# Gathering the slots' rows of h by indirect DMA instead of by a product with a selection matrix, in a four-layer graph kernel

## The chip, the cores and the metric

The kernel runs on one core of a Trainium2 chip. The metric is the device time of one execution in microseconds (us). Runs of one kernel agree within about 0.3%.

## What is computed

The inputs are node features `x` (8 batches, 2048 nodes, 64 features), a sparse row-normalised 2048 x 2048 matrix `adj`, a hypergraph membership matrix `H` (2048 nodes, 64 edges) and weights. Four layers follow each other, each as x = layernorm(x + layer(x)). The change lies in layer 1, cut here to what matters:

```python
h = x @ W
agg = einsum('ben,bnf->bef', alpha, h)              # one row per edge
beta = sigmoid((h @ a_gn)[:, None, :] + (agg @ a_ge)[:, :, None])
all_he = elu(beta * h + (1 - beta) * agg)           # node x edge pairs, where H > 0
industry = einsum('nm,bmf->bnf', adj / deg, x @ W_ind)
g = einsum('bne,benf->bnf', coefs1, all_he)         # sum over the edges of a node
out = softmax-weighted sum of industry and g        # then residual and layernorm
```

Layer 0 is a polynomial in `adj` with weights of its own per node, layers 2 and 3 are products with `adj` and small matrices.

## The kernel before

**Tiles.** The 2048 nodes are 16 tiles of 128. A row of a node holds all 8 batches x 64 features, 512 numbers, so a tile of features is 128 x 512. `j` is the tile. Matrices with `adj` are done as a 0/1 mask times a high and a low part of the features (fp32r), 32 matmuls of 128x512 a tile.

**Stages.** First product (0 to about 140 us of the span), layer 0 (to about 650), the head of layer 1 (650 to 663), its 16 tiles interleaved with each other and with layer 2's projections (663 to about 930), layer 2, layer 3.

**Units of a node.** Most nodes belong to one to three edges. A tile therefore handles four units of 128 rows each: the first, second and third edge of every node, and a fourth unit of up to 128 *slots* in which further edges of any node of the tile are listed. `S[:, j, :]` is the 0/1 matrix from nodes to slots of tile `j`; `oh` holds the 0/1 matrices from edges to the rows of each unit. Both are built in the first product by `memberships` (steps interleaved between matmuls, with one PSUM bank `li`), kept in device memory, and loaded again in layer 1.

**Steps of layer 1.** For tile `j`, `units` gives: `sx` (TensorE: gate sums and the transpose of S), `ST`, `gates`, `tau` (sigmoids `sig` and `rest`), `ch0`/`ch1` (GpSimd: sig x h, for units 0 and 1, and for unit 2), `gp0`/`gp1` (TensorE: agg of each unit, two units each), `m0`/`m1` (VectorE: times `rest`), `z0`/`z1` (VectorE: sum), `exp0`/`exp1` (ScalarE), `e0`/`e1` (VectorE: elu), `w0`/`w1` (GpSimd: times coefficient), `a0`, `ga` (GpSimd) and `red` (TensorE: slots back to nodes), `g` (VectorE). For the fourth unit the kernel before does it otherwise than for the others: `dp` (TensorE) forms h of the slot's node minus agg of its edge by two products, with S in full fp32 and with `nagg` = -agg; `t3` (ScalarE, eight pieces) multiplies this by `sig`; `m1` leaves the fourth unit out; `z1` adds agg. `mixer` holds what follows `g` (`tr`, `sT`, `fc`, `th`, `sub`, `df`, `rw`, `rt`, `mult`, `r`, `s`, `centre`, `sq`, `var`, `rstd`, `x2`), `layer2` the projections (`f`, `xT`, `mm`, `hi`, `add`, `lo`), and `industry` the mask loads (`mask`), eight portions `i` of four matmuls for each tile, and `ind`.

**Order.** Inside `program_order` every compute engine runs its instructions in the order in which they are written. For layer 1 that order is a list of some 1000 tokens (`3.gp0` is step `gp0` of tile 3) which `perform` walks through; a shorter list, `head`, orders the part on edges before it. TensorE's portions `i` are spread between the steps. SP's queue carries nearly all DMAs, in its own order, and its instructions wait in line. PSUM: `g` and `fc` have one buffer of two banks each, `m` two buffers, `sm` one.

**Lines.** L954, L955 `dp`; L960 `t3`; L944 `m`; L947 `z`; L966 `e`; L971 `w`; L925 `ch`; L936 `gp`; L985 `red`; L807 the products with `pT` in the head (`dnp`, `dnp2`); L1937 the industry products; L709, L710 the loads of `pT` and S; L1599 ScalarE's copy of `h`; L538 a write of 2048 numbers to device memory by GpSimd's queue (`s_row`).

Of the kernel before, what the change touches and what calls it, by code (L numbers as in the profile page):

```python
# [13 lines left out]
ALU = mybir.AluOpType  # L14
# [49 lines left out]
def kernel(  # L64
# [242 lines left out]
    s_row = scr.tile([1, N], F32, tag="s_row", name="s_row")  # L307
    lists = {
# [8 lines left out]
    def memberships(pre, ps, pm, fcw_sb, fcb_sb, fcg_sb):  # L317
# [23 lines left out]
        nc.gpsimd.tensor_scalar(iota[:, 1, :], iota[:, 0, :], 4.0, None, op0=ALU.add)  # L341
        cnt3, base3, end3 = (
# [34 lines left out]
        for q in range(NQ):  # L377
# [19 lines left out]
            S = pre.tile([P, 4, P], F32, tag="S", name=f"S_{q}")  # L397
            yield
            for t in range(4):
# [16 lines left out]
                for h in range(2):  # L416
                    nc.vector.scalar_tensor_tensor(
                        r_(rk[:, h, :]), sm[:, 0:E], base3[:, j:j + 1], pm[:, j, :],
                        op0=ALU.add, op1=ALU.mult,
                    )  # L420
# [8 lines left out]
                )  # L429
            store(q, oh23, 2)  # L430
            nc.sync.dma_start(lists["S"][q], S)
# [178 lines left out]
    def layer1(  # L610
# [13 lines left out]
        agg1, nagg = (  # L624
            l1.tile([P, BC], F32, tag=f"agg{i}", name=f"agg_{i}") for i in range(2)
        )
# [17 lines left out]
        def industry(j):  # L644
# [25 lines left out]
            return dict(mask=mask, i=products, ind=scaled)  # L670

        g_of, ind_of, mask_of, acc_of, done_of = {}, {}, {}, {}, {}
# [24 lines left out]
        def column_view(src):  # L697
# [3 lines left out]
            "1.mask 2.mask 3.mask 4.mask 0.i c.hexp c.he 0.ind c.w1 c.trhe c.agg1 c.heT "  # L701
            "c.w2 c.fche c.sums c.the c.nagg 1.i c.sep 1.i c.serow c.sert 1.i c.ese c.eexp c.ese2 "
            "c.dnp c.ext 1.i c.rec c.hgr c.dnp2 1.i c.late "
        )
        with tc.tile_pool(name="fa", bufs=2) as fa:
# [18 lines left out]
            with program_order():  # L724
# [46 lines left out]
                def negated():  # L771
                    full = fa.tile([P, BC], F32, tag="full", name="full", bufs=1)
                    nc.vector.tensor_scalar(full, c["agg"], -1.0, None, op0=ALU.mult)
                    parts(nagg, full)

# [54 lines left out]
                def other_weights():  # L830
# [7 lines left out]
                    agg1=lambda: parts(agg1, c["agg"]), sums=sum_edges, nagg=negated, ese=capped,  # L838
# [22 lines left out]
        def units(j, dst):  # L861
# [79 lines left out]
            def lessen(i):  # L941
                n = 2 - i
                v = by_b(gps[i][:, 0:n])
                nc.vector.tensor_tensor(v, v, per_b(t["rest"], 2 * i, n), ALU.mult)  # L944
# [7 lines left out]
            def dp():  # L952
                t["dp"] = ps_m.tile([P, BC], F32, tag="m", name=f"dp_{j}")
                nc.tensor.matmul(t["dp"], S[:, j, :], h_sb[:, j, :], start=True, stop=False)  # L954
                nc.tensor.matmul(t["dp"], r_(t["oh"][:, 3, :]), r_(nagg), start=False, stop=True)  # L955

            def t3():
                for b in range(B):
                    bc = slice(b * C, (b + 1) * C)
                    nc.scalar.activation(  # L960
                        ds[1][:, 1, bc], t["dp"][:, bc], AF.Copy, scale=t["sig"][:, 3, b:b + 1]
                    )
# [24 lines left out]
            def g():  # L987
# [4 lines left out]
                sx=sx, ST=copy_ST, gates=gates, tau=tau, dp=dp, t3=t3, a0=add0, ga=add1, red=red, g=g  # L992
# [187 lines left out]
        with program_order():  # L1180
            perform(
                (
                    "0.xr 1.xr c.rests 0.sx 0.gp0 0.ST 0.gates 0.gp1 0.tau 1.sx 0.ch0 0.m0 1.i 1.ST "
                    "0.dp 1.gates 0.ch1 0.m1 1.tau 1.i 0.z0 1.ch0 0.t3 1.dp 1.i 0.exp0 0.z1 2.sx "
                    "1.ind 0.e0 0.exp1 2.i 2.gates 1.ch1 2.ST 1.gp0 0.e1 2.tau 2.i 0.w0 1.t3 1.m0 "
                    "1.gp1 2.i 1.m1 0.w1 1.z0 2.i 0.a0 2.i 1.exp0 0.red 1.z1 0.ga 3.sx 1.e0 1.exp1 "
                    "2.dp 0.g 3.ST 2.ch0 2.gp0 1.e1 0.tr0 2.i 0.sT0 2.m0 1.w1 0.tr1 0.fc0 3.gates "
                    "0.sT1 2.z0 3.tau 2.i 2.ch1 0.th0 1.red 1.w0 2.exp0 0.fc1 2.t3 0.dlt 2.i 0.xg "
                    "2.xr 4.sx 0.th1 3.dp 1.a0 4.gates 2.ind 4.ST 0.sub 3.i 1.ga 2.e0 3.i 0.df 1.g "
                    "3.ch0 2.gp1 0.rw 1.tr0 2.m1 0.rt 3.i 1.sT0 2.w0 2.z1 4.tau 1.tr1 3.i 2.exp1 "  # L1190
                    "1.dlt 1.fc0 1.sT1 2.a0 2.e1 3.i 1.th0 0.mult 2.w1 3.gp0 0.r 1.fc1 3.m0 3.ch1 3.i "
                    "1.th1 0.s 2.ga 3.z0 3.t3 3.i 1.sub 1.xg 3.xr 3.i 5.mask 3.exp0 2.red 0.centre "
                    "3.ind 3.e0 1.df 0.sq 4.i 1.rw 2.g 4.ch0 0.var 3.gp1 2.tr0 3.m1 4.i 2.sT0 3.w0 "
                    "3.z1 2.fc0 3.exp1 4.i 2.dlt 0.rstd 2.th0 3.e1 1.rt 4.i 1.mult 2.tr1 2.xg 4.xr "
                    "0.x2 4.gp0 1.r 4.i 3.w1 4.m0 5.sx 2.sT1 1.s 4.i 5.ST 4.z0 4.ch1 4.dp 5.gates "
                    "3.a0 4.exp0 4.i 1.centre 4.t3 3.ga 4.e0 2.fc1 4.i 6.mask 4.w0 1.sq 5.tau 1.var "
                    "4.gp1 4.ind 3.red 4.m1 2.th1 5.ch0 4.z1 6.sx 5.dp 6.ST 2.sub 4.exp1 4.a0 5.i 3.g "
                    "1.rstd 4.e1 3.tr0 5.i 3.sT0 6.gates 5.gp0 4.w1 1.x2 2.df 5.m0 3.tr1 5.i 5.z0 "
                    "5.ch1 2.rw 3.fc0 3.sT1 6.tau 3.dlt 5.exp0 2.rt 4.ga 4.red 5.t3 5.e0 5.i 3.xg "
                    "5.xr 4.g 5.i 3.th0 6.ch0 2.mult 5.gp1 2.r 4.tr0 5.i 5.m1 4.sT0 5.w0 2.s 4.tr1 "  # L1200
                    "5.z1 5.i 4.xg 6.xr 7.sx 2.centre 5.exp1 5.i 7.mask 7.gates 5.a0 7.ST 2.sq 6.dp "
                    "5.e1 7.tau 5.ind 3.fc1 2.var 5.w1 6.gp0 4.sT1 6.i 3.th1 6.m0 6.ch1 5.red 3.sub "
                    "5.ga 6.t3 6.i 6.z0 2.rstd 4.fc0 5.g 6.exp0 6.i 4.dlt 5.dlt 2.x2 5.tr0 6.i 6.e0 "
                    "3.df 7.ch0 5.sT0 6.gp1 3.rw 6.i 4.th0 6.m1 6.z1 3.rt 6.w0 6.i 3.mult 4.fc1 "
                    "6.exp1 3.r 5.xg 7.xr 8.sx 4.th1 6.e1 6.i 6.a0 8.ST 4.sub 7.gp0 6.i 8.mask 6.w1 "
                    "7.m0 5.fc0 6.ind 8.gates 7.ch1 7.i 7.z0 8.tau 4.df 6.ga 3.s 7.exp0 7.i 3.centre "
                    "4.rw 7.dp 7.e0 5.th0 4.rt 7.t3 7.i 7.w0 4.mult 7.gp1 4.r 7.i 3.sq 7.m1 8.ch0 4.s "
                    "5.tr1 7.z1 7.i 5.sT1 5.fc1 7.a0 4.centre 7.exp1 3.var 7.i 5.th1 7.e1 3.rstd "
                    "6.red 4.sq 5.sub 8.gp0 7.w1 7.i 3.x2 8.m0 5.df 6.g 7.i 9.mask 8.ch1 5.rw 8.z0 "
                    "6.tr0 7.ind 7.ga 5.rt 8.dp 4.var 6.sT0 8.exp0 5.mult 6.xg 8.xr 6.fc0 5.r 8.t3 "  # L1210
                    "8.e0 8.i 4.rstd 9.sx 6.th0 5.s 6.dlt 8.gp1 9.ST 8.i 8.w0 5.centre 4.x2 9.gates "
                    "6.tr1 8.i 8.m1 6.sT1 8.a0 8.z1 7.red 9.tau 5.sq 8.i 9.ch0 7.g 8.exp1 5.var 7.tr0 "
                    "8.i 8.e1 7.sT0 7.xg 9.xr 10.sx 9.gp0 8.w1 10.gates 10.ST 9.dp 9.m0 10.tau 6.fc1 "
                    "9.ch1 9.z0 8.red 6.th1 8.ga 8.i 9.exp0 6.sub 5.rstd 11.sx 9.t3 9.e0 8.i 8.g "
                    "7.fc0 10.ch0 11.ST 5.x2 11.gates 9.gp1 8.i 10.mask 9.m1 9.w0 9.z1 11.tau 6.df "
                    "8.ind 7.tr1 8.tr0 6.rw 7.dlt 9.exp1 9.i 9.a0 6.rt 8.sT0 9.e1 9.i 7.sT1 8.xg "
                    "10.xr 7.th0 8.tr1 6.mult 10.gp0 9.w1 6.r 9.i 10.m0 7.fc1 6.s 10.ch1 9.i 8.sT1 "
                    "10.z0 7.th1 9.ga 9.red 6.centre 10.exp0 9.i 7.sub 6.sq 12.sx 10.e0 9.i 12.ST 9.g "
                    "11.ch0 10.gp1 12.gates 9.i 10.m1 9.tr0 6.var 10.w0 8.fc0 7.df 9.sT0 8.dlt 6.rstd "
                    "9.i 11.mask 7.rw 8.th0 7.rt 10.dp 7.mult 9.ind 10.a0 6.x2 7.r 10.i 7.s 8.fc1 "  # L1220
                    "9.dlt 10.t3 7.centre 9.xg 11.xr 10.i 9.tr1 8.th1 10.i 10.z1 11.dp 9.sT1 8.sub "
                    "10.exp1 10.i 7.sq 10.e1 9.fc0 12.tau 7.var 10.w1 11.gp0 10.i 11.m0 8.df 11.ch1 "
                    "11.z0 10.i 8.rw 9.th0 10.ga 8.rt 10.i 8.mult 11.exp0 7.rstd 9.fc1 8.r 11.t3 "
                    "11.e0 10.i 12.mask 8.s 12.ch0 11.gp1 9.th1 8.centre 10.red 10.ind 11.m1 12.dp "
                    "8.sq 9.sub 11.w0 7.x2 11.i 11.z1 13.sx 11.a0 10.g 11.exp1 11.i 13.gates 10.xg "
                    "12.xr 13.ST 10.tr0 11.e1 13.tau 11.i 10.sT0 8.var 11.w1 12.gp0 11.i 12.m0 10.fc0 "
                    "12.ch1 12.z0 11.i 11.ga 12.t3 10.tr1 11.i 10.dlt 8.rstd 12.exp0 11.red 10.sT1 "
# [47 lines left out]
    def layer0(  # L1275
# [334 lines left out]
        def project(j, n):  # L1610
            projected(j, n)
            for what in ("hi", "h", "sc", "lo"):
                copied(j, n, what)
# [1116 lines left out]
```

## Time and profile before

| | |
|---|---|
| runs | 1195.62, 1195.90, 1199.13 us (median 1195.9) |
| profiled execution | 1195.65 us, span 1193.9 us, granted clock 0.997 |
| TensorE busy | 1176.7 us (99%) |
| VectorE busy | 886.7 us (74%) |
| GpSimd busy | 501.5 us (42%) |
| ScalarE busy | 392.4 us (33%) |
| DMA moved | 157.1 MB, mean 132 GB/s |

Busy time is the sum of the instructions' times; matmuls are pipelined, and their records overlap. A wait that the profile shows is the idle time in front of an instruction and what ended it. Stages differ, so shares are read by window.

### The profile page before, as it was taken

Reading aid. Unit: us, or ns where it says so; the run is one execution under the profiler, and the core shown is the slowest. Engines: PE = TensorE matmul, PEld = TensorE weight load, DVE = VectorE, ACT = ScalarE, POOL = GpSimd, SP = SyncE. Lnnn points to the kernel's source line nnn. Section 1 sums busy time; section 2 is a strip of 40 time slices with the busy share of each in tenths; the row PEclk is TensorE's granted clock in tenths of the full one; section 3 lists DMA queues with packets and bytes.
Section 4 is the critical chain, followed back from the end, with each engine's and each line's share of the span. In section 5 each row is a group of like instructions: output and inputs, shape, how many; then the busy total and the mean of one; then the engine's idle time right before and its main releaser. Section 6 shows DMA issues by size and latency. Waiting matters only on the chain.

```text
span 1193.9 us, 19895 instructions
## 1 busy us (share of the span) xinstructions
PE 1176.7 (99%) x7498; PEld 942.9 (79%) x7498; DVE 886.7 (74%) x1678; ACT 392.4 (33%) x1019; POOL 501.5 (42%) x443
## 2 busy tenths in 40 slices
PE   9999999999999999999999999999999999999996
PEld 7878888888888888888887666666667888888885
DVE  4556578898888888888877788988977666665554
ACT  3100102222222222222223567767767311111111
POOL 2000392555555555555511589988860211100000
PEclk9999999999999999999999999999999999999998
DMA  8887653323333332333294223322220423325551
GB/s 288 237 253 226 171 166 100 108 102 116 109 118 117 99 99 101 111 117 116 89 344 127 70 80 106 115 76 93 97 71 1 177 106 134 113 106 177 179 180 66
DMA packets 101992, 157.10 MB, mean 132 GB/s; under 512 B 13057, under 2 KB 64641, under 8 KB 96257
## 3 DMA queue, kind: packets, MB, share of 16 engines
q1 hardware_dynamic: 97088, 151.51, 38.8%
q10 hardware_dynamic: 4368, 4.20, 1.0%
q8 instruction: 61, 1.00, 0.3%
q14 instruction: 43, 0.34, 0.1%
q0 software_dynamic: 432, 0.05, 0.1%
HBM read 117.97 MB, written 37.76 MB: 130 GB/s over the span
## 4 chain that ended last, share of the span: by engine, by line
PE 94%; DVE 3%; DMA 1%; ACT 1%; issue 1%; POOL 0%; SPq 0%; ACTq 0%; DVEq 0%; POOLq 0%
PE pp L1457 27%; PE a L1937 19%; PE ind L1937 10%; PE y1p L567 9%; PE y2p L1411 9%; PE fc L1035 3%; PE yp L2036 1%; PE try L168 1%; PE gp L936 1%; PE trm L168 1%; PE u L1146 1%; PE red L985 1%; PE hp L1582 1%; PE dp L954 1%; DVE r L1468 1%; PE df L691 1%
## 5 line engine op out<-in xcount | busy, mean ns | idle before, releaser
L1468 DVE SCALAR_TENSOR_TENSOR r<-pp,emb_sb,r 128x256 f32<-128x256 f32 x512 | 247.4, 483 | 76.0 <-PE pp L1457 61.8
L1457 PE MATMUL pp<-w_sb,xT 64*128 64x256 f32 x1024 | 155.6, 380 | 1.9 <-DVE r L1468 1.9
L1457 PE MATMUL pp<-w_sb,y2T 64*128 64x256 f32 x1024 | 153.5, 376 | 0.5 <-DVE y2T L1427 0.5
L1457 PE MATMUL pp<-w_sb,y1T 64*128 64x256 f32 x1024 | 153.4, 376 | 0.0
L1323 POOL TENSOR_TENSOR ms<-msk,srow 128x1024 f32<-128x1024 f32 x30 | 76.6, 2553 | 90.1 <-DVE msk L447 90.1
L1457 PEld LDWEIGHTS pp<-w_sb,y2T 64*128 64x128 f32 x1024 | 99.4, 187 | 11.9 <-DVE y2T L1427 0.9
L1457 PEld LDWEIGHTS pp<-w_sb,y1T 64*128 64x128 f32 x1024 | 99.4, 187 | 11.1
L1457 PEld LDWEIGHTS pp<-w_sb,xT 64*128 64x128 f32 x1024 | 95.1, 187 | 14.6 <-issue 4.4
L567 PE MATMUL y1p<-x_hi,m 128*128 128x512 f32 x256 | 103.3, 404 | 0.3 <-ACT x_hi L469 0.3
L567 PE MATMUL y1p<-x_lo,m 128*128 128x512 f32 x256 | 100.4, 392 | 0.2 <-DVE x_lo L470 0.2
L1937 PE MATMUL a<-y_lo,mj_l 128*128 128x512 f32 x240 | 95.0, 396 | 0.0
L1937 PE MATMUL a<-y_hi,mj_l 128*128 128x512 f32 x240 | 95.0, 396 | 0.0
L1411 PE MATMUL y2p<-y_hi,msk 128*128 128x512 f32 x240 | 94.8, 395 | 0.0
L1937 PE MATMUL a<-v_hi,mj_l 128*128 128x512 f32 x240 | 93.9, 392 | 0.0
L1937 PE MATMUL a<-v_lo,mj_l 128*128 128x512 f32 x240 | 93.7, 391 | 0.0
L1411 PE MATMUL y2p<-y_lo,msk 128*128 128x512 f32 x240 | 93.5, 390 | 0.0
L1937 PE MATMUL ind<-y_hi,mj_l 128*128 128x512 f32 x208 | 90.5, 435 | 0.0
L1937 PE MATMUL ind<-y_lo,mj_l 128*128 128x512 f32 x208 | 81.8, 393 | 0.0
L1363 DVE SCALAR_TENSOR_TENSOR ms<-ms,adj 128x1024 f32<-128x1024 f32 x30 | 67.2, 2240 | 0.0
L971 POOL TENSOR_TENSOR ez<-ez,coef 128x1024 f32<-128x1024 f32 x32 | 61.6, 1927 | 11.0 <-DVE ez L966 10.9
L1118 POOL TENSOR_TENSOR r<-r,bias_sb 128x512 f32<-128x512 f32 x14 | 17.9, 1277 | 105.3 <-DVE r L2057 105.3
L1649 POOL TENSOR_TENSOR hs<-h,es 128x512 f32<-128x512 f32 x15 | 15.6, 1043 | 107.9 <-ACT hgr L1621 107.9
(352 smaller groups left out, 2461.5 us busy)
## 6 DMA issues: line engine op xcount, KB each, us to landing
mj_l<-mask SPq DMA_DIRECT2D x44, 1024.0 KB, 5.0
adj<-in_at SPq DMA_DIRECT2D x64, 256.0 KB, 3.7
mask<-msk SPq DMA_DIRECT2D x32, 512.0 KB, 4.6
raw<-in_at SPq DMA_DIRECT2D x31, 512.0 KB, 5.9
oh<-oh SPq DMA_DIRECT2D x32, 128.0 KB, 4.1
xT<-in_xt SPq DMA_DIRECT2D x16, 256.0 KB, 3.1
xs<-in_xn SPq DMA_DIRECT2D x16, 256.0 KB, 2.7
kept<-x SPq DMA_DIRECT2D x16, 256.0 KB, 3.7
```

What stands on the lines that cost most here:

```text
L168: nc.tensor.matmul(dst, src, ident, start=True, stop=True, is_transpose=True)
L567: nc.tensor.matmul(accs[q][jj], r_(m[:, t, jj * P:(jj + 1) * P]), r_(part[:, mt, :]), start=i + h + t == 0 and part is x_hi, stop=i == 3 a ...
L971: nc.gpsimd.tensor_tensor(by_b(ezs[i]), by_b(ezs[i]), per_b(t["coef"], 2 * i, 2), ALU.mult)
L1035: nc.tensor.matmul(fcs[i][:, h, :], fcw_sb[rs], t["sT", i][rs], start=True, stop=True)
L1118: nc.gpsimd.tensor_tensor(b_view(t), b_view(t), bias2_sb.unsqueeze(1).to_broadcast([P, B, C]), ALU.add)
L1323: nc.gpsimd.tensor_tensor(ms, m, srow[j].unsqueeze(1).to_broadcast([P, 8, P]), ALU.mult)
L1363: nc.vector.scalar_tensor_tensor(ms, ms, 1.0, raws[j][h], op0=ALU.mult, op1=ALU.not_equal, accum_out=bad[:, 2 * j + h:2 * j + h + 1],)
L1411: nc.tensor.matmul(acc, r_(msk[j, mt // 8][:, mt % 8, :]), r_(part[:, mt, :]), start=mt == 0 and part is y_hi, stop=mt == NT - 1 and part ...
L1457: nc.tensor.matmul(pp[:, h, pl, :], terms[j][name][rs, 2 * bq + pl], w_sb[rs, k, dq * 4 * C:(dq + 1) * 4 * C], start=k == 0, stop=k == K - 1,)
L1468: nc.vector.scalar_tensor_tensor(rb, ppv[:, :, dd, :], emb_sb[:, j, d:d + 1], rb, op0=ALU.mult, op1=ALU.add)
L1649: nc.gpsimd.tensor_tensor(b_view(hs), b_view(h_sb[:, j, :]), bcast(es[:, j, :]), ALU.mult)
L1937: nc.tensor.matmul(acc, r_(a[:, mt, :]), r_(part[:, mt, :]), start=mt == 0 and part is hi, stop=mt == NT - 1 and part is lo,)
```

## The change

`h` of every tile is also stored in device memory (`h_rows`, 2048 x 512). In `memberships`, one of the two equal halves of `rk` becomes the node's number, so that the product that gives the edge ranks of the slots also gives, in its first row, the node of each slot; ScalarE writes these as integers, and they are kept in device memory as `slot_row`. Layer 1 loads them as `slot_of`, and a new step `hg` lets GpSimd's queue fetch the 128 rows of a tile's slots by an indirect DMA into one of two buffers. `dp` and `nagg` are gone, `t3` reads the fetched rows, and `m1` multiplies both of its units by `rest`. Both lists of steps are other ones. The core of the diff:

```diff
+    slot_row = scr.tile([1, N], mybir.dt.int32, tag="slot_row", name="slot_row")
+    h_rows = scr.tile([N, BC], F32, tag="h_rows", name="h_rows")
...
+        node = pre.tile([P, 1], F32, tag="node", name="node")
+        nc.gpsimd.iota(
+            node, pattern=[[0, 1]], base=0, channel_multiplier=1,
...
                 rk = pre.tile([P, 2, E], F32, tag="rk", name=f"rk_{j}")
-                for h in range(2):
-                    nc.vector.scalar_tensor_tensor(
-                        r_(rk[:, h, :]), sm[:, 0:E], base3[:, j:j + 1], pm[:, j, :],
-                        op0=ALU.add, op1=ALU.mult,
-                    )
+                nc.vector.tensor_copy(r_(rk[:, 0, :]), node.to_broadcast([P, E]))
+                nc.vector.scalar_tensor_tensor(
+                    r_(rk[:, 1, :]), sm[:, 0:E], base3[:, j:j + 1], pm[:, j, :],
+                    op0=ALU.add, op1=ALU.mult,
+                )
...
+                nc.scalar.activation(
+                    slots[0:1, t * P:(t + 1) * P], sm[0:1, P:2 * P], AF.Copy, bias=float(j * P)
+                )
             store(q, oh23, 2)
+            nc.sync.dma_start(slot_row[:, q * QW:(q + 1) * QW], slots)
...
-        agg1, nagg = (
-            l1.tile([P, BC], F32, tag=f"agg{i}", name=f"agg_{i}") for i in range(2)
-        )
+        agg1 = l1.tile([P, BC], F32, tag="agg", name="agg_1")
+        slot_of = l1.tile([P, NT], mybir.dt.int32, tag="slot", name="slot_of")
+        nc.sync.dma_start(slot_of, slot_row.rearrange("o (t p) -> p (o t)", p=P))
...
+            def slot_rows():
+                rows_of[j] = l1.tile([P, BC], F32, tag="hg", name=f"hg_{j}", bufs=2)
+                nc.gpsimd.indirect_dma_start(
+                    rows_of[j], None, h_rows,
+                    bass.IndirectOffsetOnAxis(slot_of[:, j:j + 1].bitcast(mybir.dt.uint32), 0),
+                )
...
-            "1.mask 2.mask 3.mask 4.mask 0.i c.hexp c.he 0.ind c.w1 c.trhe c.agg1 c.heT "
-            "c.w2 c.fche c.sums c.the c.nagg 1.i c.sep 1.i c.serow c.sert 1.i c.ese c.eexp c.ese2 "
-            "c.dnp c.ext 1.i c.rec c.hgr c.dnp2 1.i c.late "
+            "1.mask 2.mask 3.mask 4.mask 0.hg 0.i c.hexp 1.hg c.he 0.ind c.w1 c.trhe c.agg1 "
+            "c.heT c.w2 c.fche c.sums c.the 1.i c.sep 1.i c.serow c.sert 1.i c.ese c.eexp c.ese2 "
+            "c.dnp c.ext c.dnp2 c.rec c.hgr 1.i c.late "
...
-                n = 2 - i
-                v = by_b(gps[i][:, 0:n])
-                nc.vector.tensor_tensor(v, v, per_b(t["rest"], 2 * i, n), ALU.mult)
+                v = by_b(gps[i])
+                nc.vector.tensor_tensor(v, v, per_b(t["rest"], 2 * i, 2), ALU.mult)
...
-            def dp():
-                t["dp"] = ps_m.tile([P, BC], F32, tag="m", name=f"dp_{j}")
-                nc.tensor.matmul(t["dp"], S[:, j, :], h_sb[:, j, :], start=True, stop=False)
-                nc.tensor.matmul(t["dp"], r_(t["oh"][:, 3, :]), r_(nagg), start=False, stop=True)
...
-                        ds[1][:, 1, bc], t["dp"][:, bc], AF.Copy, scale=t["sig"][:, 3, b:b + 1]
+                        ds[1][:, 1, bc], rows_of[j][:, bc], AF.Copy, scale=t["sig"][:, 3, b:b + 1]
...
+        def kept_rows(j):
+            nc.sync.dma_start(h_rows[j * P:(j + 1) * P, :], h_sb[:, j, :])
```

The list of steps, a piece of it from the middle of tile 4, before and after (all of it is replaced):

```diff
-                    "0.x2 4.gp0 1.r 4.i 3.w1 4.m0 5.sx 2.sT1 1.s 4.i 5.ST 4.z0 4.ch1 4.dp 5.gates "
-                    "3.a0 4.exp0 4.i 1.centre 4.t3 3.ga 4.e0 2.fc1 4.i 6.mask 4.w0 1.sq 5.tau 1.var "
+                    "2.dlt 3.w1 0.var 4.gp0 2.th0 4.i 4.m0 1.rt 4.i 6.mask 4.ch1 4.z0 3.red 0.rstd "
+                    "4.ind 1.mult 4.exp0 5.i 1.r 4.t3 6.sx 4.e0 3.ga 5.i 6.gates 5.ch0 6.ST 4.gp1 "
```

In the new list a gather `j.hg` stands one to two tiles ahead of `j.t3`; `kept_rows(j)` follows the second half of `project(j)` in layer 0, on SP's queue; the load of `slot_of` stands in front of the loads of `pT` and S.

## Prediction before the run

> **What bounds the kernel now.** I read the page's first two parts first: who is busy overall, and whether that changes along the span.
>
> ```profile
> PE 1176.7 (99%) x7498; PEld 942.9 (79%) x7498; DVE 886.7 (74%) x1678; ACT 392.4 (33%) x1019; POOL 501.5 (42%) x443
> ...
> POOL 2000392555555555555511589988860211100000
> ```
>
> TensorE is busy in 99% of the span, so over the whole run work taken off it is time. But the average hides one stage: GpSimd, 42% over the run, stands at 8 to 9 tenths in slices 23 to 29. That is layer 1, the stage that the change rewrites. So I asked for busy time by windows there; columns are window, length, then PE, PEld, DVE, ACT, POOL busy, with instruction counts in brackets.
>
> ```profile
> 677.50:877.00 199.50, 199.26 (x958) 126.44 (x958) 177.19 (x268) 146.34 (x373) 174.67 (x124) 1.00 0.28 94
> ...
> 720.00:740.00 20.00, 19.82 (x95) 12.44 (x94) 17.65 (x31) 14.70 (x41) 19.42 (x15) 1.00 0.41 149
> ```
>
> The stretch 677.5 to 877 runs from the first `red` to the last `dp`: TensorE full, VectorE 88.8%, GpSimd 87.6%. GpSimd's fullest 20 us are 97%. The clock is 1.00, so no throttling takes part. TensorE has the shortest slack, yet two engines stand only 22 and 25 us behind it. Whatever is taken off TensorE here is worth at most what these two allow, and the change gives work to both.
>
> The waits in this stretch say how they hang together:
>
> ```profile
> POOL d L925 <- DVE ez L966: 11.2, 9, 2.5
> POOL ez L971 <- DVE ez L966: 10.9, 7, 4.2
> DVE gp L944 <- PE gp L936: 6.7, 9, 1.5
> ```
>
> GpSimd's 24.8 us of idle time are mostly waits for VectorE's `e`, nine and seven times; it is not free time at one place.
>
> **What is removed: `dp`.** Groups by line and form give 16.5 us for the product with S and 12.7 for the one with `nagg`, but records of pipelined matmuls overlap. The timeline shows what the sequence pays, from the start of `dp` to the start of what follows:
>
> ```profile
> 666.85 1.02 PE L954 MATMUL dp<-h,S 128*128 128x512 f32 x2
> 667.31 0.79 PE L955 MATMUL dp<-agg,oh 128*128 128x512 f32 x1
> 667.94 0.40 PE L1937 MATMUL ind<-y_hi,mp_l 128*128 128x512 f32 x1
> ```
>
> 667.94 - 666.85 = 1.09 us, 16 times: 17.4 us, of which 14 (15.3 us) lie in the stretch. TensorE alone would need 199.5 - 15.3 = 184.2 us there. Also gone are `negated`'s three VectorE instructions in the head (0.42, 0.43 and 0.69 us), which lie under the edge chain's waits for TensorE and ScalarE: taken as 0.
>
> **What is added, engine by engine.** The groups that price it (mean ns of one behind the comma):
>
> ```profile
> L944 DVE TENSOR_TENSOR gp<-gp,rest 128x1024 f32<-128x1024 f32 x16 | 19.6, 1226 | 3.5 <-PE gp L936 3.2 <-ACT rest L905 0.3
> L944 DVE TENSOR_TENSOR gp<-gp,rest 128x512 f32<-128x512 f32 x16 | 11.1, 693 | 3.5 <-PE gp L936 3.5
> L1922 POOL DMA_DIRECT2D et<-in_bias x8 | 4.3, 546 | 0.0
> L538 POOL DMA_DIRECT2D s_row<-s x1 | 1.2, 1169 | 3.2 <-DMA s<-in_at 3.2
> ```
>
> VectorE: `m1` now scales two slots instead of one, the second form becomes the first: 1.226 - 0.693 = 0.533 us, 14 times in the stretch: 177.19 + 7.5 = 184.7 us. That is already as much as TensorE's 184.2.
>
> GpSimd: 14 gathers (`hg` 2 to 15; 0 and 1 are in the head, where GpSimd waits 15.3 us for the first `sig`). The trace has no indirect DMA. Its own direct ones cost 0.546 us (16 rows), 0.786 (512 elements, L534) and 1.169 (2048 elements). A gather of 128 rows writes fewer pieces than the last, but has to fetch its row numbers first. I take 1.17 and keep 0.55 and, upward, GpSimd's slowest group of all (L1323, 2.55 us) as ends; below zero is excluded, since it is an added instruction. 174.67 + 14 x 1.17 = 191.1 us: more than TensorE's or VectorE's new need. So GpSimd becomes the one that sets the pace: `red` on TensorE waits for `w1` on GpSimd, `z` on VectorE for `ch`, and behind a gather on its queue stand just these `ch`, `w`, `ga`.
>
> How full can an in-order GpSimd be? 97% is its best slice, 87.6% its mean today with TensorE in the lead. I take 94%: its partners are now full too, and waits for `ez` go on. 191.1 / 0.94 = 203.3 us for the stretch that took 199.5: +3.8. The new order of steps does not get around this sum: `hg` stands among the same GpSimd steps, and up to `red` of tile 14 TensorE's instructions shrink while GpSimd's grow.
>
> Here a rule of the Trainium skill speaks against the change. The trace first: in this stretch `w` takes 1.895 us at least and 1.905 in the median, 2.348 at most, so GpSimd is seldom held up by VectorE. The page "SBUF — State Buffer", section "SBUF: two separate sides" with its box on the trap that DVE blocks DMA, says that GpSimd can't write the descriptors of its DMAs while a two-port VectorE instruction runs, and, one section on ("A bandwidth-pool intuition that's wrong"), that a DMA of about 620 ns then took 3100. By its figures, an estimate, the stretch would be 174.67 + 14 x 0.62 = 183.4 or 174.67 + 14 x 3.1 = 218.1 us. VectorE's instructions in the stretch are mainly two-input ones with an operand in PSUM, which that page does not count among the two-port ones, so I keep to the rows.
>
> ScalarE: `t3` reads SBUF instead of PSUM (332 ns a piece now; `x2`, the same shape from SBUF, 350): 0 to +0.14 us a tile, on an engine with 53 us of slack: 0. In the first product 16 small copies of a slot row (nearest row 128x128, 273 ns: at most 4.4 us) share the single list bank with VectorE's comparison, which runs at the same time; TensorE's 4.5 us of idle time in the first 190 us are not there. Price 0 to 4.4, I take 0. `rk`'s copy in place of one of two equal instructions, and one iota: 0.
>
> SP and DMA: 16 stores of 256 KB in layer 0, each behind ScalarE's copy of `h` on SP's queue, where the stores of `i` already wait for the same projection: 0 while the DMA share is 34 to 39%; without that cover 256 KB at the 390 GB/s of the reload of `i` is 0.66 us each. The gathers' traffic is the same 4 MB at a share of 28%: hidden, if issued two tiles ahead.
>
> The head: the table of slots is read in 2048 pieces of 4 bytes, on SP's queue in front of `pT`, S and `oh`. The nearest rows: 2048 pieces of 64 bytes landed in 5.8 us, 2048 elements written by `s_row` in 13.0.
>
> ```profile
> 649.70 0.48 SPq L709 DMA_DIRECT2D pT<-pT  x1
> ...
> 658.84 0.58 PE L807 MATMUL dnp<-ese,pT 64*128 64x16 f32 x4
> ```
>
> `pT` has 9.1 us from issue to use and lands in 4.0. With 5.8 in front it is about there in time; with 13.0 it is at least 3.9 us late (13.0 - 9.1) and its own tail, say 4.4. I take the middle, +2.2. The two `dp` outside the stretch give 2 x 1.09 = 2.2 back.
>
> **Sum:** 1195.65 (profiled execution, span 1193.9) + 3.8 + 2.2 - 2.2 = 1199.5; the median of the runs is 0.25 above that execution: 1199.7, so 1200. About 0.3% (3.6 us) is what a measurement of this kernel can tell from no change.
>
> **Rivals.**
> - *TensorE's saving comes through.* For it: TensorE leads in every window. Against: two others at 88%. With a gather of 0.79 us GpSimd needs 185.7, VectorE 184.7; at 97% the stretch is 191.5: -8.0, with the two `dp` outside -2.2, no delay in the head: 1185.4, 1186 in the median. If nothing but TensorE counted, 1195.9 - 17.4 = 1178.5. It decides from a price of the gather below (0.94 x 199.5 - 174.67) / 14 = 0.92 us at 94%, or 1.35 at 97%. Chance 0.33.
> - *It cancels:* the gather near that price, 1192.3 to 1199.5. Chance 0.22.
> - *My forecast,* GpSimd sets the pace: 1199.5 to 1213, the end with 2.55 us: (174.67 + 35.7) / 0.97 = 216.9, +17.4. Chance 0.33.
> - *The slot table is late:* 13.0 us as `s_row` had: +4.4 instead of +2.2 and S and `oh` behind it late too, another +4: 1206. Chance 0.07.
> - *A gather waits in the queue:* it has two buffers and so waits for `t3` two tiles before, and `ch` and `w` stand behind it. 14 waits of 1.2 us, as GpSimd's for `ez` now (11.2 / 9), add 17: 1217. Chance 0.05.
>
> Faster 0.33, same 0.22, slower 0.33 + 0.07 + 0.05 = 0.45. The likeliest case's own range is 1199.5 to 1213; the range over all cases goes from 1183 (a little under the first rival) to 1217 (the last).
>
> **What the changed profile would show.** Right: no L954 group; a GpSimd DMA group x16 near 1.2 us; GpSimd 93 to 95% in the stretch and TensorE with 15 to 20 us of idle time there, before `red` and `gp`, released by GpSimd's `ez` and by VectorE. Wrong: gathers under 0.8 us and TensorE still at 99% (first rival), or TensorE idle before `dnp` and `sx` near 660 us (slot table), or waits of GpSimd on ScalarE's `d` before each gather. The price of a gather is the number that I trust least; the fill of 94% comes next.

## The result and the profile after

| | before | after |
|---|---|---|
| median of 8 runs each | 1196.88 us (1195.62 to 1199.13) | 1202.48 us (1199.54 to 1205.98) |
| ratio | | 1.0048, 95% interval 1.0035 to 1.0061 |
| profiled execution, its span | 1195.65, 1193.9 us | 1201.89, 1200.2 us |

The change costs 5.6 us in the medians and 6.3 us between the two profiled spans. Executions of one kernel differ with the clock that TensorE was granted: on the chip of experiments 1 to 4 the kernel before took 1193.4 to 1195.9 us in 16 executions with a mean clock of 0.997 or 0.998 (the profiled one is of this kind) and 1196.2 to 1199.4 in ten with 0.993 or 0.994, while the kernel after never had more than 0.992. The forecast was 1200, by GpSimd setting the pace in layer 1. The time is near it. The cause is not.

First the page of the kernel after: busy time, then GpSimd and the granted clock in 40 slices.

```profile
PE 1168.3 (97%) x7450; PEld 941.4 (78%) x7450; DVE 891.4 (74%) x1675; ACT 400.0 (33%) x1035; POOL 516.9 (43%) x460
...
POOL 2000284545555555555531499999982211100000
PEclk9989999999999999999999899999999999999999
```

TensorE is busy 8.4 us less, half of what `dp` took, and the span is longer all the same. GpSimd shows 9 in six slices of layer 1, as forecast. The line PEclk has two new dips of the clock, in slices 3 and 23: one in the first product, one in the head of layer 1.

To see where the time went I cut the span at three marks that both kernels have: the last transposes of layer 0 (`trx_last`), and the first and the last `w` of layer 1 (tile `ez` on GpSimd). From the answers on these tiles, before and then after (count, min/median/max in ns, first and last start in us):

```profile
L168 PE MATMUL trx_last<-ident,x x4: 273/274/327, 641.5 to 645.9; 128*128 128x128 f32 x4
L971 POOL TENSOR_TENSOR ez<-ez,coef x32: 1895/1905/2348, 673.4 to 885.5; 128x1024 f32<-128x1024 f32 x32
```

```profile
L168 PE MATMUL trx_last<-ident,x x4: 273/284/328, 650.6 to 655.1; 128*128 128x128 f32 x4
L979 POOL TENSOR_TENSOR ez<-ez,coef x32: 1892/1904/2217, 686.5 to 896.0; 128x1024 f32<-128x1024 f32 x32
```

| part, us | before | after | difference |
|---|---|---|---|
| start to the end of layer 0 | 645.9 | 655.1 | +9.2 |
| head: from there to the first `w` | 27.5 | 31.4 | +3.9 |
| first `w` to last `w` | 212.1 | 209.5 | -2.6 |
| last `w` to the end of the span | 308.4 | 304.2 | -4.2 |

So layer 1, where the forecast saw the loss, became a little shorter, although 24 of its industry products that stood behind the last `w` before now lie in front of it (392 of them in the stretch before, 416 after). The loss stands at a place where the sum had a zero: ahead of layer 1. There is one wait there that the kernel before does not have. The timeline of the kernel after (in brackets: idle time of the engine ahead, and what ended it):

```profile
79.71 0.70 DVE L537 TENSOR_SCALAR m<-raw 128x1024 fp32r<-128x1024 f32 x1 [5.18 <-DMA raw<-in_at]
80.43 0.29 DVE L435 TENSOR_TENSOR oh<-sm,iota 64x128 fp32r<-64x128 f32 x1
80.81 0.27 ACT L438 ACTIVATE slots<-sm 1x128 int32<-1x128 f32 x1 [8.45 <-issue]
81.13 0.42 PE L412 MATMUL sm<-tri,pT 128*128 128x64 f32 x1 [5.84 <-ACT slots L438]
...
81.94 0.63 PE L579 MATMUL y1p<-x_lo,m 128*128 128x512 f32 x1
...
86.06 0.39 PE L579 MATMUL y1p<-x_lo,m 128*128 128x512 f32 x1
```

Read upward from TensorE: `sm` waits 5.84 us for ScalarE's copy, which starts when VectorE's `oh` has ended (80.43 + 0.29 = 80.72), and `oh` stands in VectorE's queue behind the mask `m`, which waits for a piece of `adj`. ScalarE is only the last link, 0.3 us long. Afterwards a product takes 0.63 us instead of 0.39 for 4 us. The granted clock, 1.00 throughout the first product before, is 0.94, 0.72 and later 0.83 in three windows of 10 us (70 to 90, 150 to 160). Of the 9.2 us, 6.8 stand at the last product `y1p` (it starts at 141.0 us instead of 134.2); the rest comes with a second wait and the second fall of the clock behind it:

```profile
154.12 1.22 PE L1465 MATMUL pp<-w_sb,y2T 64*128 64x256 f32 x4 [2.79 <-DVE y2T L1435]
```

Why the piece is late, SP's own timeline shows, before and after:

```profile
67.13 0.60 SPq L242 DMA_DIRECT2D w_sb<-in_w  x1
68.17 0.33 SPq L522 DMA_DIRECT2D raw<-in_at  x1
70.13 2.53 SPq L351 DMA_DIRECT2D oh<-oh  x4
```

```profile
67.14 0.44 SPq L442 DMA_DIRECT2D slot_row<-slots  x1
68.08 0.46 SPq L389 DMA_DIRECT2D pT<-pT  x1
68.60 0.58 SPq L242 DMA_DIRECT2D w_sb<-in_w  x1
70.71 2.53 SPq L358 DMA_DIRECT2D oh<-oh  x4
73.34 1.20 SPq L366 DMA_DIRECT2D pT_raw<-in_hypt  x2
74.59 2.09 SPq L534 DMA_DIRECT2D raw<-in_at  x4
```

Before, the next piece of `adj` is issued at 68.17, in front of four stores of `oh`. After, a store of `slot_row` stands at 67.14, SP's whole order behind it is another, and the piece is issued at 74.59, behind the four stores and two loads. The store itself takes SP only 0.44 us, so it is the order and not its length that makes 6.4 us.

Theory A: this order of SP's queue costs the 9.2 us. Its rival A': ScalarE's copy in the release of the single list bank does. Theory B: the forecast, GpSimd's pace in layer 1. For what layer 1 does by itself, theory C (GpSimd) stands against D (VectorE, or the order of steps).

### The profile page after: what moved, and what is told of

Its sections match the earlier page's. It is cut to its first block, busy times and chain, and to the rows that moved or that the text cites. A ratio compares the mean times of both kernels' runs of the same rounds, so it can differ in the third digit from the quotient of the medians.

```text
span 1200.2 us, 19910 instructions
## 1 busy us (share of the span) xinstructions
PE 1168.3 (97%) x7450; PEld 941.4 (78%) x7450; DVE 891.4 (74%) x1675; ACT 400.0 (33%) x1035; POOL 516.9 (43%) x460
## 4 chain that ended last, share of the span: by engine, by line
PE 77%; DVE 7%; POOL 4%; DMA 4%; ACT 4%; issue 2%; SPq 1%; DVEq 0%; POOLq 0%; ACTq 0%
PE pp L1465 27%; PE a L1952 19%; PE y2p L1419 9%; PE y1p L579 7%; PE ind L1952 3%; PE yp L2051 1%; PE try L168 1%; PE fc L1043 1%; DMA xraw<-in_xn 1%; POOL ez L979 1%; PE hp L1590 1%; DMA s_row<-s 1%; PE u L1154 1%; DVE ez L974 1%; POOL d L939 1%
## 5 line engine op out<-in xcount | busy, mean ns | idle before, releaser
L1952 PE MATMUL a<-v_lo,mj_l 128*128 128x512 f32 x240 | 93.7, 391 | 0.0
```

The costliest lines, as they stand in the source:

```text
L1952: nc.tensor.matmul(acc, r_(a[:, mt, :]), r_(part[:, mt, :]), start=mt == 0 and part is hi, stop=mt == NT - 1 and part is lo,)
```

## The experiments

Each group was timed beside the kernel before on one chip; ratios go against that. All trace numbers are of one profiled execution each.

| kernel | median, us | before, us | ratio, 95% interval |
|---|---|---|---|
| slot stores on GpSimd's queue | 1190.75 | 1195.12 | 0.9958, 0.9942 to 0.9974 |
| slots by VectorE | 1201.75 | 1195.12 | 1.0039, 1.0022 to 1.0056 |
| before, plus slot rows | 1204.18 | 1195.12 | 1.0065, 1.0043 to 1.0087 |
| slot_of on GpSimd's queue too | 1190.36 | 1195.12 | 0.9956, 0.9939 to 0.9973 |
| table stored turned | 1194.17 | 1195.53 | 0.9977, 0.9964 to 0.9991 |
| gather twice | 1206.80 | 1195.53 | 1.0099, 1.0076 to 1.0123 |
| no gather | 1191.60 | 1195.53 | 0.9960, 0.9944 to 0.9975 |
| m1 short | 1190.38 | 1195.53 | 0.9947, 0.9928 to 0.9966 |
| head spread | 1191.06 | 1196.38 | 0.9954, 0.9937 to 0.9971 |
| lists of before | 1203.43 | 1196.38 | 1.0057, 1.0037 to 1.0076 |
| no gather, m1 short | 1188.77 | 1197.46 | 0.9921, 0.9905 to 0.9937 |
| slot_of behind the head's small steps | 1192.23 | 1197.46 | 0.9951, 0.9937 to 0.9966 |

### 1. The slot stores on GpSimd's queue

```diff
-            nc.sync.dma_start(slot_row[:, q * QW:(q + 1) * QW], slots)
+            nc.gpsimd.dma_start(slot_row[:, q * QW:(q + 1) * QW], slots)
```

> The changed kernel with one edit: the four stores of slot_row leave on GpSimd's queue instead of SP's. SP's queue in the first product then has the order of the kernel before; ScalarE's copies stay. Theory A (the time is lost in the first product, because SP's new order fetches a piece of adj late: TensorE idles 5.8 us at 75 us and multiplies at a lower clock for some 9 us after it; the traces stand 645.75 against 654.92 us at the end of layer 0, 9.2 us apart): the end of layer 0 comes back to 646 +/- 1, the kernel to 1202.5 - 9.2 = 1193.3 us, so faster than before by 3 to 4 us. Theory A' (same place, but it is ScalarE's copy in the release of the list bank that stalls TensorE): the stall stays, 1200 to 1203. Theory B (the recorded forecast: GpSimd's pace in layer 1 costs the time, the first product nothing): 1202 +/- 1.

The kernel falls to 0.9958 of before, from 1.0048. `trx_last` starts last at 647.2 instead of 655.1, and the longest wait before `sm` is 1.2 us, though ScalarE's copies are still there. That is theory A, with about a per cent (1.0048 - 0.9958 = 0.0090, 10.8 us) for four small stores on the wrong queue: SP's order in the trace is that of before again (a piece of `adj` at 68.96, in front of the four stores of `oh`). No run kept the stores on SP and forced that order. Theory B expected 1202. Its single executions spread from 1187.1 (mean clock 0.998) to 1196.7 (0.991); the profiled one is the slowest.

### 2. The slot rows by VectorE

```diff
-                nc.scalar.activation(
-                    slots[0:1, t * P:(t + 1) * P], sm[0:1, P:2 * P], AF.Copy, bias=float(j * P)
-                )
+                nc.vector.tensor_scalar(
+                    slots[0:1, t * P:(t + 1) * P], sm[0:1, P:2 * P], float(j * P), None, op0=ALU.add
+                )
```

> The changed kernel with one edit: VectorE instead of ScalarE writes the slot rows (behind its comparison on the same bank). The stores stay on SP, in the same late order of the first product. Theory A (SP's order): the stall before the next product of the list bank stays, 1202 +/- 2. Theory A' (ScalarE in the release of the list bank): it goes, 1193 to 1196. Theory B: 16 small VectorE copies more, 1202 to 1204.

The stall stays, now with VectorE's own copy as its last link:

```profile
80.66 0.39 PE L412 MATMUL sm<-tri,pT 128*128 128x64 f32 x1 [5.68 <-DVE slots L438]
```

So A' falls: which engine copies the rows does not matter while SP's order is this one.

### 3. The kernel before with the slot rows alone

The edit is the part of the diff in `memberships` (`node`, `rk`, `slots`, and the store of `slot_row` on SP's queue); layers 0 to 3 are those of before.

> The kernel before plus only the first product's part of the change: rk's first half is the node number, ScalarE writes the slot rows, SP stores them (nothing reads them); layers 0 to 3 as before, dp included. Theories A and A': the end of layer 0 is 9 us later, 1196.9 + 9 = 1205 to 1206 us. Theory B: 1196 to 1198, as before.

The full loss without anything of layer 1: 1.0065, +9.1 us in the medians. The trace has the wait again (4.85 us before `sm`) and the end of layer 0 late:

```profile
L168 PE MATMUL trx_last<-ident,x x4: 272/284/330, 652.2 to 656.6; 128*128 128x128 f32 x4
```

656.6 - 645.9 = 10.7 us. Head and `w` stretch are those of before (27.5 and 212.2 us), the rest is 306.6 instead of 308.4. These 1.8 us, between two kernels that are the same there, say how far one execution's rest can be trusted.

### 4. The load of slot_of off SP as well

```diff
-        nc.sync.dma_start(slot_of, slot_row.rearrange("o (t p) -> p (o t)", p=P))
+        nc.gpsimd.dma_start(slot_of, slot_row.rearrange("o (t p) -> p (o t)", p=P))
```

> The first of these kernels (stores of slot_row on GpSimd's queue) with one edit more: the load of slot_of also leaves on GpSimd's queue, so that SP issues pT, S and oh about 0.5 us earlier, as in the kernel before. If the wait of TensorE for oh at the start of layer 1 (1.75 us, and 10 us at a lower clock behind it, some 4 us) comes from the table's place on SP: the wait goes and the time is 2 to 5 us below the first kernel, 1189 to 1191. If it comes from the table's 2048 pieces on the DMA engines themselves, or if the wait costs nothing in the end: within 1 us of the first kernel.

In the time nothing (0.9956 after 0.9958), so the second branch by the numbers. In the profiled executions the head is shorter (28.5 us after 31.2): the wait for `oh` is gone, but a new one of 1.36 us stands before `trhe`: the load takes GpSimd 1.26 us in front of `minus1`, which ScalarE needs for the exp of the edges. One wait was exchanged for another. Experiment 12 takes that up.

### 5. The table stored turned

```diff
-    slot_row = scr.tile([1, N], mybir.dt.int32, tag="slot_row", name="slot_row")
+    slot_row = scr.tile([P, NT], mybir.dt.int32, tag="slot_row", name="slot_row")
...
+            nc.gpsimd.dma_start(
+                slot_row[:, 4 * q:4 * q + 4].rearrange("p t -> t p").unsqueeze(0),
+                slots.rearrange("o (t p) -> o t p", p=P),
+            )
...
+        nc.sync.dma_start(slot_of, slot_row)
```

> The kernel with the stores of slot_row on GpSimd's queue, and one edit more: the table is stored turned (128 x 16, in pieces of 4 bytes, in the first product), so that its load in front of pT, S and oh is 128 pieces of 64 bytes instead of 2048 of 4. That kernel's executions went from 1187 to 1197 us (median 1190.8); its profile has a wait of TensorE for oh of 1.5 us at the start of layer 1 and then 12 us at half the clock. If the table's pieces delay oh: no wait, no half clock, 1186 to 1188 us. If it is only the table's place on SP: as that kernel, 1190 to 1192. If the turned stores hurt the first product: above 1192.

It got worse, to 0.9977: the last branch. A store of 512 pieces takes GpSimd 1.12 us instead of 0.54 and lands in 7.9 us instead of 4.0, and the next `slots` buffer waits for it; `sm` waits four times, 4.8 us. Its head tells something else. TensorE has no wait in the 5 us ahead of it here, and yet the clock halves, directly behind the 16 small products that the new list puts in one row. Timeline:

```profile
664.74 0.39 PE L1955 MATMUL ind<-y_lo,mp_l 128*128 128x512 f32 x1
665.15 2.23 PE L824 MATMUL dnp<-ese,pT 64*128 64x16 f32 x16
667.31 0.80 PE L1955 MATMUL ind<-y_hi,mp_l 128*128 128x512 f32 x1
667.90 0.63 PE L1955 MATMUL ind<-y_lo,mp_l 128*128 128x512 f32 x1
```

### 6 to 8 and 11. What layer 1's additions cost

All on the base of 5. The kernels without the gathers and with the short `m1` leave out part of the layer; they serve to price it. Gather twice and no gather:

```diff
+                again = l1.tile([P, BC], F32, tag="hg2", name=f"hg2_{j}", bufs=1)
+                nc.gpsimd.indirect_dma_start(
+                    again, None, h_rows,
+                    bass.IndirectOffsetOnAxis(slot_of[:, j:j + 1].bitcast(mybir.dt.uint32), 0),
+                )
```

```diff
-                nc.gpsimd.indirect_dma_start(
-                    rows_of[j], None, h_rows,
...
+                rows_of[j] = h_sb[:, j, :]
```

> The kernel with the turned table, and each gather issued twice (the second into a buffer that nothing reads): 16 more GpSimd instructions of 1.09 us, 14 of them in the full stretch of layer 1. Theory C (the forecast's: GpSimd, 94% busy there, sets the pace): +14 x 1.09 = 15.3 us, a little more with the fill: +12 to +17. Theory D (VectorE, 93% busy, or TensorE's chain sets it): +0 to +5, as far as GpSimd's idle time goes (180 - 168.5 = 11.5 us in 700 to 880).

> The kernel with the turned table without any gather: t3 reads the tile's own rows of h instead of the slots' rows (so the values of the fourth unit are other ones). 16 x 1.09 = 17.4 us less on GpSimd, 15.3 of it in the stretch. Theory C: TensorE takes the lead back, -5 to -9 us against the kernel with gathers (the rest of the 17.4 us that dp gave back). Theory D: -0 to -2.

`m1` short, and both at once:

```diff
-                v = by_b(gps[i])
-                nc.vector.tensor_tensor(v, v, per_b(t["rest"], 2 * i, 2), ALU.mult)
+                n = 2 - i
+                v = by_b(gps[i][:, 0:n])
+                nc.vector.tensor_tensor(v, v, per_b(t["rest"], 2 * i, n), ALU.mult)
```

> The kernel with the turned table, gathers kept, but m1 scales only the third unit as in the kernel before (the fourth unit's rest is left out of the result): 16 x 0.533 = 8.5 us less on VectorE. Theory C: -0 to -2 against the kernel with the turned table, GpSimd stays at its work. Theory D: -5 to -8.

> The kernel with the turned table, without the gathers (t3 reads the tile's own rows of h) and with the short m1 (the fourth unit's rest left out): 17.4 us less on GpSimd and 8.5 us less on VectorE at once. Alone they gave 2.6 and 3.8 us. If GpSimd and VectorE hold the pace together (each at 93 to 94%), both at once give more than the sum: 8 to 12 us against the kernel with the turned table (1194.2), so 1182 to 1186. If their effects only add: 1187 to 1189. If something else (ScalarE, the order of the list) holds the rest: not below 1189.

Against the base of 1194.17: twice +12.6, none -2.6, short -3.8, both -6.7 (0.9921/0.9977 x 1194.2 = 1187.5). The first set of gathers costs 2.6 us and a second one 12.6, for 17.4 us of GpSimd each: a knee, not a slope. The second set is what theory C said (12 to 17). In the medians both additions together give about the sum of the two (6.4), but these differences are known to some 2.5 us by the intervals, so the 8 to 12 of a joint pace is not excluded. The stretch from first to last `w` speaks rather for it: 210.3 us in the base, 208.5 without gathers, 209.2 with the short `m1` (with 3.4 us at half clock in it) and 204.2 with both: -1.8 and -1.1 alone, -6.1 together. These are single executions, so whether the two engines hold the pace jointly stays open. -2.6 and -3.8 can't be told apart either, so I rank neither engine first. Theories C and D are both too simple.

Busy time between the first and the last `w`, in four kernels: before, after, gather twice, and without both (columns: window, length, PE, PEld, DVE, ACT, POOL, clock, DMA share, GB/s):

```profile
673.40:885.50 212.10, 211.66 (x1016) 133.97 (x1014) 187.76 (x279) 155.29 (x400) 183.00 (x131) 1.00 0.27 90
```

```profile
686.50:896.00 209.50, 203.23 (x990) 131.49 (x989) 192.43 (x275) 158.12 (x396) 194.75 (x143) 1.00 0.33 108
```

```profile
677.00:900.80 223.80, 206.27 (x990) 131.77 (x989) 196.75 (x275) 158.56 (x398) 209.66 (x156) 0.99 0.35 118
```

```profile
674.80:879.00 204.20, 201.46 (x983) 130.42 (x983) 183.03 (x275) 157.22 (x394) 181.32 (x129) 1.00 0.27 93
```

GpSimd's fill: 86.3%, 93.0%, 93.7%, 88.8%. Between one gather a tile and two the fill hardly rises any more and the stretch grows by 14.3 us (13.5 against the 210.3 of its own base). The waits with two gathers show GpSimd holding up VectorE's `g`, and through it TensorE's `trm`, and `red`; in the kernel after the first and the last are missing and the second is 0.5 us:

```profile
DVE g L1004 <- POOL g L997: 5.3, 2, 2.8
PE trm L168 <- DVE g L1004: 4.8, 3, 2.4
PE red L1001 <- POOL ez L987: 2.9, 2, 1.6
```

Here GpSimd is at its limit. With one gather it is filled almost as far. Before, it had room.

In the last kernel TensorE's work is shorter by the whole of `dp`: its busy time from the end of layer 0 to the end of the span is 536.4 us before and 519.4 there, 17.0 less. Of these, 12.6 us come back as time: the stretch falls from 548.0 to 535.4.

### 9. The head spread

```diff
-            "c.dnp c.ext c.dnp2 c.rec c.hgr 1.i c.late "
+            "c.dnp c.ext 1.i c.rec c.hgr c.dnp2 1.i c.late "
...
-                    "0.gp1 0.m0 1.tau 2.sx 0.ch1 1.i 2.ST 0.z0 1.ch0 0.t3 1.i 0.m1 1.i 0.exp0 2.hg "
+                    "0.gp1 0.m0 1.tau 2.sx 0.ch1 1.i 2.ST 0.z0 1.ch0 0.t3 1.i 0.m1 0.exp0 2.hg "
```

> The kernel with the slot stores and the load of slot_of on GpSimd's queue, and one edit more: in the head, one portion i of four large products goes back between the first 4 and the other 12 small products with pT, and one in front of tile 0 (as in the list of before); one portion i less behind, in tile 1. In the profiles of the changed kernel and of its variants the granted clock falls to 0.50 for 3 to 16 us at that place, in one (the turned table) directly behind the 16 small products without any wait ahead of them; in the kernel before it never falls there. Theory H (it is the row of small products and short waits that takes the clock down): the clock stays at 1.00 there, the time from the end of layer 0 to the end falls from 542.5 to about 540, and the kernel by 2 to 4 us, to 1187 +/- 1.5. Theory W (it is the wait for oh): that kernel has no such wait already, so nothing changes, 1190 +/- 1.

0.9954 beside 0.9956 of its base: nothing to see. Behind the small products the clock now stays at 1.00, but the portion taken from tile 1 leaves a wait of 2.1 us for `ind` behind it, and the clock halves there (0.63 in 672 to 676). The edit made a hole of its own, so it does not decide between H and W; what exactly takes the clock down stays open.

### 10. The lists of before

Every `j.dp` of the old body becomes `(j+1).hg`, the head is the old one without `nagg`; base is kernel 4.

> The same base (slot stores and slot_of on GpSimd's queue) with both lists of steps of the kernel before: dp of tile j is replaced by hg of tile j + 1, the gather for tile 0 and nagg's place in the head aside. This shows what the operations alone do without the new order. Theory C (GpSimd and VectorE, both near 94% in 700 to 880, set the pace whatever the order): within 3 us of the base, 1188 to 1193. Theory O (the new order is what loses the rest of dp's 17.4 us): 1180 to 1186. If the old order leaves gathers waiting on GpSimd's queue behind t3 (hg 2 stands directly behind t3 of tile 0): 1194 to 1200, and GpSimd waits for ScalarE's d before the gathers.

1203.43, 1.0057 beside 0.9956: the old order costs the same operations 1.0%, some 12 us. None of the three branches said so. Theory O was right that the order matters and wrong in the sign: it expected the old order to be faster, and the new order is what lets the change pay. The last branch came nearest, but the waits of GpSimd before gathers, on which it rested, are 0.5 us, and `t3` does not wait for a gather: not these. Which steps of the list make the difference no run shows. The `w` stretch is 221.6 us, and TensorE idles 17.2 of them. Its longest waits:

```profile
PE gp L950 <- DVE ez L974: 5.3, 7, 1.8
PE ind L1945 <- ACT ind L678: 4.2, 6, 1.3
PE trm L168 <- DVE g L996: 2.3, 2, 1.8
```

In the kernel after, with the new order, TensorE idles 6.3 us in the same stretch:

```profile
PE gp L950 <- DVE ez L974: 2.1, 3, 1.3
PE df L710 <- DVE th L1055: 1.8, 3, 0.7
PE ind L1952 <- ACT ind L678: 0.8, 1, 0.8
```

### 12. slot_of behind the head's small steps

The load of experiment 4, moved behind `minus1`, `mhalf` and `av32` on GpSimd's queue.

> The kernel with the slot stores and the load of slot_of on GpSimd's queue, with the load behind GpSimd's three small instructions of the head instead of in front of them. In the trace of that kernel the load (1.26 us on GpSimd) stands in front of minus1, for which ScalarE's exp of the edges waits (1.9 us), then VectorE's he and TensorE's trhe (1.4 us). If this chain is what it cost: 1.0 to 1.5 us less than 1190.4, so 1189; the wait before trhe is 0.3 us again. If the half clock behind it decides: 1187 to 1193.

0.9951 beside 0.9956: within the intervals no gain can be claimed. The trace does show the chain gone (wait before `trhe` 0.2 us) and the head clean: clock 1.00, 27.4 us from `trx_last` to the first `w`, as before's 27.5. Kernels 1, 4, 9 and 12 beat both given ones, before by 0.4 to 0.5% and after by about 1% (0.9951/1.0048 = 0.990).

## Why the time was near and the reason wrong

The four parts of the span, against before, in the kernels that tell most (us, from the same marks):

| kernel | to end of layer 0 | head | first to last `w` | rest |
|---|---|---|---|---|
| after | +9.2 | +3.9 | -2.6 | -4.2 |
| slot_of behind the head's steps | -1.0 | -0.1 | -1.1 | -4.3 |
| lists of before | -1.4 | +1.1 | +9.5 | -1.6 |
| gather twice | +1.7 | +1.9 | +11.7 | -4.0 |
| no gather, m1 short | +1.9 | -0.5 | -7.9 | -4.2 |

One trace is one execution. Kernels after, 1, 4, 5 and 12 run the same steps in layer 1 in the same order, and their `w` stretch goes from 209.5 to 212.3 us (-2.6 to +0.2), their time from the end of layer 0 to the end from 542.5 to 547.7 (-5.5 to -0.3). None comes near the +3.8 of the forecast.

Step by step through the sum:

- **`dp`, 17.4 us:** right as work taken off TensorE: 17.0 us of busy time less with no gather and `m1` short, of which 12.6 came back as time.
- **`m1`, +0.533 us each, and a gather at 1.17:** right in size. The groups after have 32 `m` of 1.227 us and 16 gathers of 1.089, landing 3.9 us after their issue in the median. Without the longer half of `m1` the kernel is 3.8 us faster, less than the 8.5 us of VectorE.

```profile
L957 DVE TENSOR_TENSOR gp<-gp,rest 128x1024 f32<-128x1024 f32 x32 | 39.3, 1227 | 4.2 <-PE gp L950 4.1
...
L684 POOL DMA_INDIRECT hg<-h_rows,slot_of x16 | 17.4, 1089 | 12.2 <-ACT d L968 5.7 <-DMA slot_of<-slot_row 4.7 <-issue 1.2
```

- **GpSimd filled to 94%:** right as a limit (93.0% after, 93.7% with two gathers). **The stretch, +3.8:** wrong; -2.6 after. Two things failed in it. The stretch that I chose, first `red` to last `dp`, had GpSimd at 87.6%; from first to last `w`, which is GpSimd's own stretch, it is 86.3%. The same sum made there, with the measured price and the 13 gathers that lie in it, gives (183.0 + 13 x 1.09) / 0.94 = 209.8, 2.3 us less than the 212.1 of before, and near the 209.5 measured (194.75 us of GpSimd, filled to 93.0%). And the sentence that the new order of steps does not get around this sum was wrong: the order decides whether that fill can be reached. With the old one GpSimd is filled to 89% (197.1 of 221.6 us) and the stretch is 9.5 us longer. I had compared sums per engine and not the order in which the engines wait for each other. The row of 11.2 us and nine waits for `ez` was of a wider window (645 to 930 us); inside the stretch it is 8.8 us and eight waits. Only the price of the last rival uses it.
- **The head, +2.2:** +3.9 after. The table lands in 3.9 us, less than the 5.8 to 13.0 that I allowed, and `pT` is in time: no wait before `dnp`. It is `oh`, behind it on SP, that TensorE waits for, and the clock halves. The wait, and then windows of 1 us (the clock is the third number from the end):

```profile
672.86 0.99 PE L885 MATMUL sx<-ext,oh 128*128 128x16 f32 x4 [1.75 <-DMA oh<-oh]
```

```profile
672.00:673.00 1.00, 0.14 (x1) 0.18 (x2) 0.00 (x0) 0.00 (x0) 0.00 (x0) 0.86 0.33 123
673.00:674.00 1.00, 1.00 (x6) 1.00 (x7) 0.00 (x0) 0.00 (x0) 0.00 (x0) 0.50 0.07 27
...
683.00:684.00 1.00, 1.00 (x6) 0.80 (x6) 0.93 (x1) 0.99 (x1) 0.75 (x1) 1.00 0.00 0
```

- **Two `dp` outside, -2.2:** the rest became 4.2 us shorter. With the new list TensorE has done the last 24 industry products of layer 1 inside the `w` stretch (some 0.23 us each, 5.5 us); with the old one, in kernels before and 10, they stand behind the last `w`. That the span would follow the stretch one to one was another tacit assumption.
- **The first product, 0 (0 to 4.4):** wrong, +9.2, and the largest term of all. The step priced the 16 copies on the list bank. The four stores of `slot_row` that go with them, on SP's queue, were in no step, and they are what moved the loads of `adj`. TensorE idled only 4.5 us there before, so a late load had nothing to hide behind.
- **Stores of `h_rows` and `t3`, 0:** right. With the slot stores off SP the end of layer 0 lies between 2.2 us behind that of before and 2.0 ahead of it (but for the profiled execution of kernel 5, +6.3, with its waits in the first product); `t3` takes 337 ns a piece instead of 332.

So two misses of opposite sign made up the sum: first product +9.2 instead of 0, and the rest -2.9 instead of +3.8. That the total came out near is luck. Of the rivals, that TensorE's saving comes through was nearer to what layer 1 does, but only with the new order and with a third of 17.4 us (5.5 from the end of layer 0 on, in kernel 12). The table that is late happened in part, as a late `oh`. The gather that waits in the queue happened five times for 5.7 us, a third of the 17 that it was given. The signs that I named were mixed: GpSimd at 93% as announced, but TensorE idle 6.3 us in the stretch instead of 15 to 20, and not at all before `red`.

The page "SBUF — State Buffer" (section "SBUF: two separate sides") says that GpSimd can't write the descriptors of its DMAs while a two-port VectorE instruction runs. The forecast was right not to price the gathers by that rule: the 16 gathers take 978, 1092 and 1325 ns (least, median, most) beside a VectorE that is busy 92% of the stretch, mainly with two-input instructions that have an operand in PSUM, and none came near 3100. No run here was made to set two-port instructions beside the gathers, so the rule itself is not tested. On the clock, the page "TensorE: Matmul & The Clock Gate" (section "HAM oscillation — how this bites in real kernels") says that idle gaps of more than about 3.4 us take it to half. The half agrees: the rows show 1.00 and 0.50. The gap does not: here a wait of 1.75 us ahead of small products was enough, and a row of small products without any wait.

## What to carry over

When an edit adds a DMA, count that DMA on its queue before anything else: here four stores of 2 KB on a shared queue cost 9 us, more than all that was changed on the compute engines, by the order that the scheduler gave to the loads behind them. When the engines' sums lie within a few per cent of each other, the sum of one engine says how far an order of steps could come and not how far it comes (12 us between two orders of the same operations); make the sum over that engine's own stretch, from its first to its last step, and ask separately whether the work behind moves up. And if the time fits, look at the parts all the same.

## What was not expected of the hardware

- The granted clock is 0.50 or 1.00 (values between are windows that hold a change), and its changes lie on a grid. Read in windows of 0.1 us, it falls and rises in the kernel after at 78.79 and 85.62, 153.89 and 157.30, 672.71 and 682.95 us: 2, 1 and 3 times 3.413 us at half clock, and the falls 22 and 174 times 3.413 us behind the first. In all twelve traces with falls the times at half clock are 3.41, 6.83, 10.24 or 13.65 us, also where TensorE was full all the while.
- What brings a fall is clear only in part. In the kernel after it came at the end of a period of this grid in which TensorE was busy for 1.8 of 3.4 us (the wait of 1.75 us for `oh`), in kernel 5 at the end of one with 16 products of 64x16 and no wait. The place on the grid may decide: kernels 4 and 12 both have waits of 0.36 or 0.37 and 0.32 us ahead of `sx`. In kernel 4 both lie in one period, and the clock falls at its end (665.77 us); in kernel 12 they lie in two, and it stays at 1.00. No run moved only that place, so this is not shown.
- A load in 2048 pieces of 4 bytes took SP 0.38 us to issue and landed in 3.9; on GpSimd's queue 1.26 and 6.4 to 7.8 us (kernels 4, 10 and 12). A store in 512 such pieces took GpSimd 1.12 us, one row of 2 KB 0.54.
- An indirect DMA of 128 rows of 2 KB holds GpSimd for 1.09 us, about as long as a direct one that writes 2048 single elements (1.17).
